# Row lists split by 64-row parts, and all-node blocks in layers 1 and 3, in a four-layer graph-attention kernel

## The chip, the cores and the metric

The kernel runs as one program on one core of a Trainium2 chip. The time of a run is the device time in microseconds, and a kernel's time is the median of its runs. The kernel before took 2251.94 us (three runs, 2251.93 to 2260.22). One execution was also profiled, and the profile's span, from the first to the last instruction, is 2249.3 us.

The engines are named as the profile names them: PE (TensorE matmuls) and PEld (its weight loads), DVE (VectorE), ACT (ScalarE), POOL (GpSimd, which here issues the indirect gathers) and SP (the queue of the plain DMAs).

## The reference

There are 4096 nodes of 256 features, and an adjacency matrix with density 1/256 plus the diagonal. Four graph-attention layers follow each other, each with a residual sum and a layer norm. Cut to what matters, layer 0 is:

```
h = (x @ W.T) in 4 heads of 64
e[i, j] = leaky_relu(alpha_src[i] + alpha_dst[j], 0.2)
attn = softmax over j of (e where adj[i, j] else -inf)
x = layernorm(x + concat over heads of attn @ h)
```

Layer 1 is the same with other weights. Layer 2 has 2 heads of 128. Layer 3 has two attentions, one of e and one of -e; both weigh x itself, the results are multiplied by a weight matrix, and an elu follows. All layers use the same adjacency.

## The kernel before

**Row tiles and lists.** The rows are worked on in 32 tiles of 128 (P = 128, NT = 32). A tile does not visit all 4096 nodes. While layer 0 runs, the generator `lists` (lines 293 to 486) finds for each row tile the nodes that are a neighbour of at least one of its 128 rows. `Block.prepare` loads the adjacency of four row tiles and turns it into bytes; `Block.places` counts where each node goes in the list; `Block.pack` compares an iota with these places (L440, one DVE operation for each of 31 node tiles) and multiplies the one-hot result with the mask on PE (L446), which moves mask columns and node numbers into up to 13 groups of 128 nodes. A fixed table, WINDOW, tells for each node tile which groups it may reach. The masks go to the DRAM tensor `maskC` and the node numbers to `idx`. A flag records whether anything fell outside; if it did, `dense_layers` computes everything again after the packed program.

**A sparse row tile.** `RowTile.load` issues the loads of a tile in two halves of 7 groups: the row factors S, the mask, the tile's own nodes (a plain DMA) and 13 indirect gathers by POOL (L647), each of which fetches one projected row for each of 128 nodes. The first six gathers read only nodes below MIX * 128 (MIX = 17). `RowTile.half` then computes the weights of 7 groups: for layers 0 and 1 one head's exponential comes as a product of two factors on DVE (L704, L708) and the three others from ACT (L712, an Exp with the node's term as bias); one DVE operation for two heads applies the lower bound and the mask (L681), with the mask copied into PSUM ahead of it (L666). The matmuls follow. Layers 0 and 1 (L724) load the 65 gathered value columns as weights and stream 128 rows, so the sums stand transposed; `copy` (L749) and `back` (L757) turn them. Layers 2 and 3 (L727) load the 128 x 128 weights and stream 129 or 257 value columns. `finish` and `norm` divide, add the residual and normalize.

**Projections.** `Projection` makes the next layer's rows: transposes (L543), products (L557), terms and values (L575 to L583), the row terms' transposition (L589).

**All-node blocks.** The table WHOLE names blocks of four row tiles that take no list: blocks 3, 7 and 6 in layer 2 and block 7 in layer 3. `whole_rows` goes through all 32 node tiles for them, with ACT exponentials of 128 x 512 (L1016), a DVE masking (L1017) and matmuls (L1027).

**The order.** There is no scheduler that moves work between steps: `Layer.part`, `half_alone`, `half_with_whole` and `close` write out the order in which each engine gets its instructions, and every engine works its queue in order. `half_with_whole` puts after each half some units of the all-node work (one unit is one node tile), spread evenly over the layer's halves by `whole`. `run` asks `lists` for one more row tile after each half tile of layer 0, ten tiles ahead (LEAD), and for the first 14 tiles' lists during layer 0's projections.

**Buffers.** Gathered rows stand in two pools: g0 with 16 and g1 with 14 buffers of two groups each. PSUM's eight banks are shared out in pools: ptwo (2 + 2), pair0 (2), pair1 (1) and pair2 (1, the mask copies).

## Time and profile before

| what | value |
|---|---|
| median of the runs | 2251.94 us |
| span of the profiled execution | 2249.3 us |
| PE busy | 2014.0 us (90%) |
| DVE busy | 1786.6 us (79%) |
| ACT busy | 1737.9 us (77%) |
| POOL busy | 1494.4 us (66%) |
| indirect gathers (L647) | 1456, mean 1017 ns |
| moved | 492.99 MB, mean 219 GB/s |

A busy share is that of the engine over the whole span, and the stages differ: layer 0 with the lists takes until about 784 us, layer 1 until 1347, layer 2 until 1763, layer 3 the rest. In a line of the view by stretches the columns are the stretch, its length, the busy time of each engine with its instructions, the granted TensorE clock, and the DMA share and rate. In a line of a timeline they are start, duration, engine, line, operation, tiles and count; in brackets stands how long the engine was idle before and what ended that. An f32 matmul is two records of the profile.

### The profile page before, as it was taken

The page shows a single profiled execution, that of the slowest core. Times are in us where ns is not written, and L with a number is a line of the kernel's source. Part 1 is how long each engine was busy: PE and PEld are TensorE (multiplying, and loading weights), DVE is VectorE, ACT ScalarE, POOL GpSimd, SP SyncE. Part 2 cuts the span into 40 slices and gives each one's busy share as a digit, 9 for nine tenths or more (in the row PEclk, how much of TensorE's full clock was granted, in tenths as well). Part 3 has the DMA queues.
Part 4 walks back from the last instruction along what each step waited for, and adds up shares of the span by engine and source line. Part 5 has one row for each costly group of instructions (what it writes and reads, how often), then busy time and mean ns, then how long its engine had stood idle before and what let it go on. Part 6 is the DMA issues. An engine that isn't in the chain of part 4 may idle for free. (4 is left out here: it accounts for less than half of the span.)

```text
span 2249.3 us, 49137 instructions
## 1 busy us (share of the span) xinstructions
PE 2014.0 (90%) x15689; PEld 1834.3 (82%) x15689; DVE 1786.6 (79%) x5060; ACT 1737.9 (77%) x4989; POOL 1494.4 (66%) x1597
## 2 busy tenths in 40 slices
PE   4878889989999969988899898989999999999995
PEld 2658788878899859988888798989998888788784
DVE  2889899999999959987988886887876566566566
ACT  4778988988789859987888776987876677667664
POOL 2107655656677777777777777777773477777773
PEclk7999999999999989999999999999999999999998
DMA  8879877777566665666665666777777688888884
GB/s 284 258 245 360 272 219 250 254 247 228 146 170 191 174 202 168 182 175 175 173 185 162 172 167 171 226 209 223 223 227 225 200 282 280 249 284 270 262 248 130
DMA packets 250319, 492.99 MB, mean 219 GB/s; under 512 B 44385, under 2 KB 156610, under 8 KB 249666
## 3 DMA queue, kind: packets, MB, share of 16 engines
q0 software_dynamic: 81536, 245.30, 38.3%
q1 hardware_dynamic: 163906, 240.26, 33.3%
q10 hardware_dynamic: 4608, 4.20, 0.5%
q8 instruction: 126, 2.06, 0.4%
q14 instruction: 143, 1.17, 0.2%
HBM read 437.05 MB, written 52.54 MB: 218 GB/s over the span
## 5 line engine op out<-in xcount | busy, mean ns | idle before, releaser
L647 POOL DMA_INDIRECT G<-vals,idx x1456 | 1480.7, 1017 | 715.7 <-issue 221.1
L712 ACT ACTIVATE w<-S,G 128x128 f32<-128x128 f32 x3248 | 1001.6, 390 | 140.6 <-DMA G<-vals,idx 101.6
L724 PE MATMUL bank<-w,G 128*65 128x128 f32 x7168 | 837.8, 276 | 59.7 <-DVE w L681 59.3
L724 PEld LDWEIGHTS bank<-w,G 128*65 128x65 f32 x7168 | 798.7, 140 | 69.9 <-DVE w L681 68.4
L681 DVE SCALAR_TENSOR_TENSOR w<-w,bank 128x1792 f32<-128x1792 f32 x256 | 514.6, 2013 | 13.4 <-ACT w L712 11.2
L727 PE MATMUL bank<-G,w 128*128 128x257 f32 (+1 forms) x2660 | 490.8, 342 | 25.7 <-ACT z L1102 13.6
L727 PEld LDWEIGHTS bank<-G,w 128*128 128x128 f32 x2660 | 431.9, 195 | 73.2 <-ACT z L1102 16.4
L1027 PE MATMUL bank<-vw,pw 128*128 128x129 f32 (+1 forms) x2048 | 298.5, 301 | 3.7 <-issue 2.3
L1027 PEld LDWEIGHTS bank<-vw,pw 128*128 128x128 f32 x2048 | 273.6, 191 | 20.1 <-issue 2.8
L690 ACT ACTIVATE w<-S,G 128x128 f32<-128x128 f32 x385 | 137.8, 393 | 136.8 <-DMA G<-vals,idx 90.0
L440 DVE TENSOR_SCALAR oh<-iota,place 128x256 bf16<-128x256 f16 (+2 forms) x992 | 221.8, 298 | 9.4 <-PE bank L446 9.1
L704 DVE TENSOR_TENSOR w<-S,G 128x256 f32<-128x256 f32 x384 | 151.9, 416 | 69.9 <-DMA G<-vals,idx 66.5
L446 PE MATMUL bank<-mk,oh 128*128 128x132 fp8e4 x2336 | 192.1, 226 | 13.8 <-ACT cm L453 7.0
L557 PE MATMUL bank<-wext,xT 128*128 128x268 f32 (+3 forms) x640 | 176.9, 409 | 16.9 <-ACT xT L548 14.1
L446 PEld LDWEIGHTS <-oh 128*128 128x128 bf16 x2336 | 146.9, 99 | 50.4 <-DVE oh L440 12.7
L385 ACT ACTIVATE mk<-raw 128x1024 uint8<-128x1024 int32 x128 | 130.5, 1051 | 28.0 <-DMA raw<-in_adjB_dram 27.7
L557 PEld LDWEIGHTS bank<-wext,xT 128*128 128x128 f32 x640 | 117.2, 200 | 36.0 <-ACT xT L548 16.9
L1017 DVE SCALAR_TENSOR_TENSOR pw<-pw,mw 128x512 f32<-128x512 f32 x192 | 127.6, 689 | 18.2 <-ACT pw L1016 17.5
L1016 ACT ACTIVATE pw<-Sw,d 128x512 f32<-128x512 f32 x192 | 133.2, 711 | 7.5 <-PE bank L1027 7.0
L714 DVE SCALAR_TENSOR_TENSOR w<-w,mk 128x896 f32<-128x896 f32 x80 | 86.6, 1086 | 41.1 <-ACT w L712 37.9
L1024 DVE TENSOR_TENSOR pw<-pw,mw 128x512 f32<-128x512 f32 x64 | 43.6, 691 | 85.4 <-ACT pw L1023 48.0
L692 DVE TENSOR_TENSOR w<-w,mk 128x896 f32<-128x896 f32 x55 | 60.0, 1091 | 59.5 <-ACT w L691 58.2
(140 smaller groups left out, 1563.3 us busy)
## 6 DMA issues: line engine op xcount, KB each, us to landing
raw<-in_adjB_dram SPq DMA_DIRECT2D x128, 512.0 KB
mk<-maskC SPq DMA_DIRECT2D x112, 231.0 KB
G<-vals,idx POOLq DMA_INDIRECT x1456
S<-edge SPq DMA_DIRECT2D x64, 256.0 KB
vw<-vals SPq DMA_DIRECT2D x96, 129.0 KB
xp<-y SPq DMA_DIRECT2D x96, 128.0 KB
y<-xp SPq DMA_DIRECT2D x96, 128.0 KB
mw<-maskW SPq DMA_DIRECT2D x20, 528.0 KB
```

Of the source, the lines that this page charges most:

```text
L440: nc.vector.tensor_scalar(oh[:, :n * P], iota[:, :n * P], self.place[:, it, j:j + 1], None, op0=ALU.is_equal)
L446: nc.tensor.matmul(accs[b][:, s * MC:(s + 1) * MC], oh[:, (k - a) * P:(k - a + 1) * P], mk[:, j, it, :].bitcast(FP8), start=touches[b][0] ...
L557: nc.tensor.matmul(pp[:, :c1 - c0], self.xT[:, k, :], wext[:, k, c0:c1], start=(k == 0), stop=(k == KT - 1 and brow is None))
L647: nc.gpsimd.indirect_dma_start(out=self.place(pos), out_offset=None, in_=sh["v"][n][:NODES[t], :], in_offset=bass.IndirectOffsetOnAxis(ap= ...
L681: nc.vector.scalar_tensor_tensor(pair, pair, LEAST, mh2, op0=ALU.max, op1=ALU.mult)
L690: nc.scalar.activation(w[0][:, k, :], S[:, 0, :], AF.Relu, bias=d(k, 0))
L704: nc.vector.tensor_tensor(w[h][:, k:k + 2, :], S[:, h:h + 1, :].to_broadcast([P, 2, P]), dd[:, :, V + T + h:V + T + h + 1].to_broadcast([P ...
L712: nc.scalar.activation(w[h][:, k, :], S[:, h, :], AF.Exp, bias=d(k, h))
L724: nc.tensor.matmul(accs[0][:Wd, h * P:(h + 1) * P], v, w[h][:, k, :], **how)
L727: nc.tensor.matmul(a, w[h][:, k, :], v, **how)
L1016: nc.scalar.activation(p, S[:, h], AF.Exp, bias=d)
L1027: nc.tensor.matmul(accs[it][:, c:c + Wd], p[:, it, :], v[:, c:c + Wd], start=(j == 0 and h == heads[0]), stop=(j == NT - 1), skip_group_ch ...
```

## The change

The list of a row tile is split by the two 64-row parts of the tile. A node that only the upper 64 rows need goes into the upper part of a *pair* unit, a node that only the lower 64 rows need into the lower part; a node that both need, or that does not fit, goes into a *mixed* unit. There are 5 pair units, each with 128 nodes for either part, and 3 mixed units. With the tile's own nodes a row tile has 9 units (U) of 128 x 128 weights instead of 14, and still 13 gathers.

```diff
-NG = 13
-NP = NG + 1
+HP = P // 2
+NPAIR = 5
+NMIX = 3
+NPACK = NPAIR + NMIX
+NU = NPACK + 1
+NP = 2 * NPAIR + NMIX
+HALF = 7
+FIRST = 3
+UNITS = (1 + FIRST, NPACK - FIRST)
+FULL = ((0,), tuple(range(NPAIR - FIRST, NPACK - FIRST)))
+PAIRS = (tuple(range(1, 1 + FIRST)), tuple(range(NPAIR - FIRST)))
...
-MIX = 17
+MIX = 23
...
-WHOLE = ((), (), (3, 7, 6), (7,))
+WHOLE = ((), (7, 6), (3, 7, 6), (7, 6))
```

`places` now sorts the nodes into three classes and computes places for each, with some 34 DVE operations a block; `pack` compares with an iota of up to 640 elements, since a node tile may reach pair units and mixed units:

```diff
-                    nc.vector.tensor_scalar(oh[:, :n * P], iota[:, :n * P], self.place[:, it, j:j + 1], None,
-                                            op0=ALU.is_equal)
-                    for k in range(a, a + n):
+                    nc.vector.tensor_scalar(oh[:, :len(ks) * P], iota[:, :len(ks) * P], self.place[:, it, j:j + 1],
+                                            None, op0=ALU.is_equal)
+                    for i, k in enumerate(ks):
```

In `half` the exponentials and factor products of a pair unit are done for 64 rows each with the part's own nodes, the maskings cover 4 or 5 units instead of 7, and all layers load the weights and stream the values. A 64-row part writes its own 64 partitions of the accumulator. `copy` and `back` go.

```diff
-        for h in heads:
-            for k in range(HALF):
...
-                v = G[k][:, h * Wd:(h + 1) * Wd]
-                if n < 2:
-                    nc.tensor.matmul(accs[0][:Wd, h * P:(h + 1) * P], v, w[h][:, k, :], **how)
-                else:
-                    a = accs[h][:, :Wd] if n == 3 else accs[0][:, h * Wd:(h + 1) * Wd]
-                    nc.tensor.matmul(a, w[h][:, k, :], v, **how)
+        for t, heads in enumerate(turns):
+            for us in (FULL[half], PAIRS[half])[::-1 if t == 1 and (half == 1 or n < 3) else 1]:
+                for h in heads:
+                    for u in us:
+                        for rows, g in parts[u]:
+                            a = accs[h][rows, :Wd] if n == 3 else accs[0][rows, h * Wd:(h + 1) * Wd]
+                            nc.tensor.matmul(a, w[h][:, u, rows], g[:, h * Wd:(h + 1) * Wd],
...
```

A new generator, `whole_heads`, does the all-node blocks of layer 1. It writes the exponential as the larger of a row factor and a node factor (the rest of the product is in the values), so that a weight is one DVE operation, and has no exponential per node tile. The row factors R stand in two PSUM banks (`pfloor`). Of two heads at a time, one loads weights and streams values, the other loads values and streams weights, and is turned at the end:

```diff
+                for h in (up, flat):
+                    R[h] = prog.bank(prog.pfloor)
+                    Sh = S[:, h].rearrange("p t i -> p (t i)")
+                    if h < A:
+                        nc.scalar.activation(R[h], Sh, AF.Exp, scale=-1.0, bias=sh["shift30"])
+                        nc.vector.tensor_scalar(R[h], R[h], HUGE, None, op0=ALU.min)
...
+                    for h in (up, flat):
+                        p[h] = prog.dp.tile([P, BT, P], F32, name="pw")
+                        nc.vector.scalar_tensor_tensor(p[h], R[h].rearrange("p (t i) -> p t i", t=BT), c[:, j, h:h + 1], mj,
+                                                       op0=ALU.max, op1=ALU.mult)
...
+                    for it in range(BT):
+                        nc.tensor.matmul(bu[:, it * Wd:(it + 1) * Wd], p[up][:, it, :],
+                                         v[:, up * Wd:(up + 1) * Wd], start=j == 0 and it == 0, **how)
+                        nc.tensor.matmul(bf[:Wd, it * P:(it + 1) * P], v[:, flat * Wd:(flat + 1) * Wd],
+                                         p[flat][:, it, :], start=j == 0 and it == 0, **how)
```

The buffers of gathered rows become larger and fewer, and while layer 1 runs its projections have one PSUM bank:

```diff
-        self.g0 = self.pool("g0", 16)
+        self.g0 = self.pool("g0", 4)
...
-        self.g1 = self.pool("g1", 14)
+        self.g1 = self.pool("g1", 4)
...
-        self.prog.banks = self.prog.ptwo[1] if self.n in (0, 2) else self.prog.pthree
+        self.prog.banks = self.prog.ptwo[1] if self.n in (0, 2) or self.closing else self.prog.pone
```

A buffer now holds 7 groups of layers 0 to 2 or 4 of layer 3. The sizes of the norm groups of layer 1 change, and layer 1 ends in the way in which layers with all-node blocks end (`close` starts all-node units of the next layer ahead of its first half).

## The prediction

> **What bounds the kernel now.** I read the busy times by stretch first, cut where one layer's gathers end and the next layer's begin (about 172, 784, 1347 and 1763 us), with one stretch inside the list building of layer 0.

> ```profile
> core 0: us, PE busy (x) PEld busy (x) DVE busy (x) ACT busy (x) POOL busy (x), PEclk, DMA share, GB/s
> 20.00:172.00 152.00, 108.11 (x956) 80.98 (x955) 113.42 (x466) 108.05 (x258) 16.15 (x58) 0.85 0.83 271
> 260.00:580.00 320.00, 286.10 (x2877) 260.65 (x2875) 314.45 (x943) 277.78 (x825) 196.05 (x193) 0.99 0.72 232
> 784.00:1347.00 563.00, 500.04 (x4196) 467.41 (x4194) 471.88 (x1083) 457.26 (x1538) 428.44 (x442) 0.97 0.63 176
> 1347.00:1763.00 416.00, 388.43 (x3055) 371.44 (x3055) 318.30 (x895) 317.06 (x857) 286.61 (x262) 0.98 0.73 212
> 1763.00:2249.00 486.00, 449.86 (x2028) 389.45 (x2026) 294.88 (x914) 314.90 (x668) 347.48 (x339) 0.96 0.80 249
> ```

> While lists are built DVE is full (314 of 320). Layers 2 and 3 are PE's (93%). In layer 1 no engine looks full, so I read POOL's timeline there, and who waited for whom.

> ```profile
> 1007.41 0.95 POOL L647 DMA_INDIRECT G<-vals,idx  x1 [0.30 <-issue]
> 1008.66 0.95 POOL L647 DMA_INDIRECT G<-vals,idx  x1 [0.30 <-PE bank L724]
> 1009.92 0.95 POOL L647 DMA_INDIRECT G<-vals,idx  x1 [0.30 <-issue]
> 1011.17 0.95 POOL L647 DMA_INDIRECT G<-vals,idx  x1 [0.31 <-issue]
> ```
> ```profile
> DVE w L704 <- DMA G<-vals,idx: 50.0, 26, 3.5
> ```

> A gather starts every 1.255 us: 0.95 busy and 0.30 of issue, whatever else runs. 13 of them are 16.3 us a row tile, and layer 1's 32 tiles, like layer 0's last eight, go at 16.4. Layer 1 is POOL's queue.

> The price of a matmul is read from starts in the PE timeline and in the chain; an f32 matmul is two records.

> ```profile
> 1006.74 6.28 PE L724 MATMUL bank<-w,G 128*65 128x128 f32 x56
> ...
> 1014.46 0.46 PE L757 MATMUL bank<-ident,aT 65*128 65x65 f32 x4
> ```
> ```profile
> 1488.73 1.50 PE L1027 MATMUL bank<-vw,pw 128*128 128x129 f32 x12
> 1490.07 0.27 PE L589 MATMUL bank<-ident,row 128*1 128x128 f32 x1
> 1490.18 0.38 PE L543 MATMUL bank<-ident,y 128*128 128x128 f32 x2
> 1490.40 1.84 PE L727 MATMUL bank<-G,w 128*128 128x129 f32 x15
> ```
> ```profile
> 1848.61 6.07 PE bank L727 x28
> 1854.68 1.73 PE bank L1027 x8
> ```

> 6.28 for 56 records (layers 0 and 1) is 0.112 with the tail, 0.109 from start to start; 1488.73 to 1490.07 for 12 is 0.112 at 129 columns; 6.07 for 28 is 0.217 at 257 columns (layer 3). A weight load hides under the record ahead in all of them. A 65-column record is seen only as a transpose, about 0.065 from start to start.

> **The change, part by part.**

> *Lists (layer 0).* A row tile still gathers 13 times, but packs into 8 units instead of 13. Per list tile the built program has 118 PE records for 73, and the same 31 DVE compares, wider: 640 elements in 341 of 992, 512 in 248, 384 in 279, 256 in 124. The forms before take 0.249, 0.291 and 0.316 us at 128, 256 and 384 elements, so about 0.35 and 0.38 at 512 and 640; consecutive DVE operations overlap by 0.07, so 31 compares go from 7.0 to 8.3 us. The placing of a block goes from 9 DVE operations to some 34, 13 of them 256 wide (0.42): 1.4 to 8.2 us a block, 0.35 to 2.05 a tile. The two halved reductions and the index arithmetic add 0.2. That is **+3.3 us of DVE a list tile.**

> *Sparse tiles of layers 0 and 1.* The maskings L681 take 2.01 at 1792 elements; with 0.69 at 512 (L1017) that is 1.03 ns an element, so 1.22 at 1024 and 1.48 at 1280: net of overlap 7.8 to 5.1 a tile. Factor products 2.5 to 1.5, mask copies 0.6 to 0.5. **-3.8 us of DVE a tile.** ACT has the same 42 exponentials, 30 of them half as wide, and loses the 0.57 copy of the transposed sums; four transposes go from PE.

> *Layer 0's sum.* In the middle stretch +3.3 and -3.8 meet on the full engine: 22 tiles by -0.5 = **-11 us**. At the start there are 14 lists and hardly a sparse tile: 14 by 3.3 = 46 us of DVE, of which the 39 us in which DVE idles between 20 and 172 can hide a part; PE gets 14 by 45 records by 0.06 = 38 more beside it. Bounds +15 to +60; I take **+35**. The last eight tiles stay at POOL's 16.4: nothing.

> *Layer 1.* Eight tiles leave POOL: 24 by 16.3 = 391 us is its new floor, so another engine is late next. PE: a sparse tile has 16 full-unit matmuls (128 weight columns, 65 streamed) and 40 of 64 weight columns. The first are bounded by 0.055 (half of 0.109, as half the columns stream) and 0.112 (L1027, same load of 128 x 128); I take 0.112, as that load has to be made. The second lie between half of 0.109 and 0.109; I take 0.065, the transpose's. 32 by 0.112 + 80 by 0.065 = 8.8 us a tile for 12.2 + 0.4 now; 24 tiles 211. Projections 2.1 by 32 = 67. The two all-node blocks: 512 matmuls with 128 weight columns (0.112 a record) and 512 of 128 streamed columns (0.109): 226, or 200 if a short record's load hides under a long one. PE 478 to 504. DVE: 14.7 - 3.8 = 10.9 by 24 = 262, the eight tiles' endings 24, 256 maskings of 512 elements 170 (0.665 net, L1017) to 190 (the row factors now lie in PSUM; 256-wide L1121 from PSUM takes 0.06 more than L1126 from SBUF), factors 8: 464 to 484. Both run side by side 93% full, as in layers 2 and 3: 563 becomes **510 (-53)**. The 18 us in which PE stands at 822 to 840 now can take all-node work, but that work first waits for the last projected tile, so I count nothing there.

> *Layer 2.* POOL's floor 326. Its sparse matmuls are 40 half-width and 16 full ones a tile. Two consecutive half-width ones stand in the two 64-column halves of the array (the built program places them at columns 0 and 64). No row shows such a pair. Its bounds: one after the other, 0.110 a record as now (no gain), or side by side, two for the time of one. Then 16 by 0.112 + 40 by 0.055 = 4.0 for 6.3 us; 20 tiles by 2.3 = 45 off PE's 388; POOL's 16.3 a tile leaves **-28** of it.

> *Layer 3.* 24 sparse tiles for 28, two all-node blocks for one (a block is 32 x 4 x 2 x 2 by 0.217 = 111). PE now 28 by 12.15 + 111 = 451. Side by side: 24 by (16 by 0.217 + 40 by 0.109 = 7.8) + 222 = 409; one after the other: 24 by 12.15 + 222 = 514. POOL's floor is 391. The bytes stay (about 137 MB), and at the 310 GB/s of the busiest stretches take 440. So **460 (-26)** side by side, **550 (+64)** one after the other. I take side by side for both layers: the two parts use disjoint columns and the trace shows loads hidden under any earlier record; both ends stay for the range.

> [...]

> *Changing array shape* costs by the rows nothing or 0.09: L589 has a 32-column tile, and starts 0.11 after the L1027 record, with the next 0.11 after it, so no pause; L560, a tile of few rows, starts 0.31 after a record of 0.22. The change alternates full and half-width matmuls some three times a half row tile, 136 halves in layers 1 to 3: 0 to 37 us. I take 0, as L589 too is a column tile.

> [...]

> **Sum.** 2249.3 + 35 - 11 - 53 - 28 - 26 = 2166; the median shown is 2.6 above the profiled span, so **2170 us**.

> **Rivals.**
> (a) *The halves don't run side by side.* The place is layer 3's PE, +64 instead of -26, and layer 2 gains nothing: +35 - 11 - 53 + 64 = 2284 + 2.6, about **2290, slower**. It decides once a pair in layer 3 takes more than about 1.7 times one record (83 of gain against a swing of 118). For it: no row shows overlap of two matmuls. Against: nothing in the program orders the two.
> (b) *The vector side of layer 1 and the longer lists eat the gain.* DVE at 484 and PE at 504 wait for each other through few buffers and one PSUM bank for projections; if layer 1 stays near 550 and the start takes 50: about **2222**. For it: layer 1's DVE is fuller than layer 3's.
> (c) *Weight loads overlap too and the start hides:* layer 1 near 480, start +5: about **2105**.
> (d) A list that overflows its window sends the program through the dense path after all, thousands of us; windows of 4.5 deviations leave that under 1 in 100.

> **Chances.** Forecast 0.50, (a) 0.25, (b) 0.15, (c) 0.09, (d) 0.01. The forecast's own range is 2125 to 2215 (start bounds, layer-1 bounds, drain). To leave out two in ten, the range goes half into (a) and (c): 2095 to 2285. Faster by over 0.5% (about what a measurement can tell from no change): 0.49 + 0.09 + 0.11 of (b) + 0.02 of (a) = 0.71; within 0.5% 0.07; slower 0.22.

> **What would show it.** Right: 28-record halves of layer 3 near 4 us instead of 6.07; layer 1's row tiles about 21 us apart with PE and DVE above 90%; POOL with idle time in layer 1; 1300 gathers still 1.255 apart; first sparse tile of layer 0 some 35 us later, its middle pace still 21 to 22. Wrong: half-width records of layer 3 starting every 0.217; pauses at each change between full and half-width; POOL still back to back in layer 1; DVE idle in the list stretch.

## The result, and the profile after

The changed kernel takes **2342.68 us** (median of four runs, 2332.35 to 2351.3) where the kernel before, run beside it, takes 2256.08: a ratio of **1.038, 95% interval 1.036 to 1.041, slower**. The forecast was 2170 and the range 2095 to 2285, so both the size and the sign were wrong. The profiled execution took 2332.35 us, its span is 2330.6.

In some sessions the engines idled on their own issue (PE for 312 to 472 us, for 0 to 26 in all others) and the kernel before itself took 2742 to 2772 us, where two of the same chips ran it in some 2256 at another time; runs from there are marked "stalling session" and are compared only with the kernel before beside them.

First the busy times by stretch of the changed kernel: list building, layer 0's middle, and layers 1, 2 and 3. (The cuts at 900, 1460 and 1856 are the first gathers of layers 1, 2 and 3. Of the cuts of before, 784 is layer 1's first gather too, but 1347 is layer 1's last finished row tile and 1763 lies 20 us behind layer 2's: there the next layer's first gathers had begun at 1313 and 1681.)

```profile
core 0: us, PE busy (x) PEld busy (x) DVE busy (x) ACT busy (x) POOL busy (x), PEclk, DMA share, GB/s
20.00:223.00 203.00, 141.88 (x1492) 116.56 (x1491) 146.38 (x562) 110.86 (x250) 17.42 (x13) 0.82 0.71 235
300.00:700.00 400.00, 335.22 (x3820) 306.26 (x3817) 341.99 (x1093) 255.99 (x843) 203.72 (x210) 0.74 0.62 192
900.00:1460.00 560.00, 504.58 (x5228) 447.33 (x5226) 456.59 (x1121) 310.80 (x1179) 304.12 (x313) 0.92 0.63 180
1460.00:1856.00 396.00, 356.32 (x3000) 327.36 (x3000) 286.38 (x871) 295.09 (x857) 274.22 (x260) 0.94 0.71 205
1856.00:2330.00 474.00, 437.92 (x2345) 322.35 (x2345) 279.41 (x906) 325.17 (x739) 320.39 (x313) 0.96 0.83 263
```

The second line is the surprise. In layer 0's middle, VectorE was 98% busy before and is 85% busy now, PE's share fell only from 89 to 84%, and the clock that PE is granted fell from 0.99 to **0.74**. Busy PE time is stretched by a low clock: the changed kernel's list records (L510) start 113 ns apart in the median where the trace's clock record says 0.5, and 59 where it says 1.0. So PE's 335 us hold, by estimate, only some 248 us of work at full clock (335 x 0.74). The page's clock row shows the stretch by eye: sevens and sixes where the kernel before had nines.

```profile
PEclk7999999999999989999999999999999999999998
PEclk8987777677678677799999997899999999999998
```

(The first row is the kernel before, the second the changed one.) A half row tile shows what that means: 28 short records of layer 0 in the PE timeline.

```profile
505.78 3.89 PE L819 MATMUL bank<-G,w 128*128 128x65 f32 x28 [2.59 <-DVE w L763]
509.60 0.38 PE L662 MATMUL bank<-ident,row 128*4 128x128 f32 x1
509.91 3.89 PE L819 MATMUL bank<-G,w 128*64 128x65 f32 x28
```

These are 3.89 us, after a wait of 2.59 for the masking. The waits of that stretch (columns: us in total, times, longest):

```profile
ACT cm L516 <- PE bank L510: 60.8, 23, 8.3
PEld bank L819 <- DVE w L763: 51.6, 29, 3.0
PE bank L819 <- DVE w L763: 45.8, 29, 2.8
DVE oh L504 <- PE bank L510: 44.7, 31, 2.3
```

PE waits for VectorE's masks (L763), VectorE waits for PE to free a compare buffer (L504), and ScalarE's list copies wait for PE too. No engine is full. In the same part of the kernel before (230 to 600 us) the two lines of PE and VectorE waiting for each other were 27 and 4 us:

```profile
PE bank L724 <- DVE w L681: 27.2, 24, 2.3
DVE oh L440 <- PE bank L446: 4.3, 1, 4.3
```

Where the 81 us of span came from, by the first and last row tile's finish in each layer (worked out from the ends of L1117 and L1127 before, L1264 and L1274 after):

| stretch | before | after | difference |
|---|---|---|---|
| start to layer 0's first finish | 210.6 | 262.6 | +52 |
| layer 0, first to last | 601.6 | 656.2 | +55 |
| layer 0's last to layer 2's first (all of layer 1) | 569.8 | 595.2 | +25 |
| layer 2, first to last | 360.7 | 331.3 | -29 |
| into layer 3 | 58.0 | 65.7 | +8 |
| layer 3, first to last | 437.2 | 410.6 | -27 |
| end | 11.4 | 9.0 | -2 |

### The profile page after: what moved, and what is told of

Its sections match the earlier page's. It is cut to its first block, busy times and chain, and to the rows that moved or that the text cites. A ratio compares the mean times of both kernels' runs of the same rounds, so it can differ in the third digit from the quotient of the medians.

```text
span 2330.6 us, 54083 instructions
## 1 busy us (share of the span) xinstructions
PE 2013.2 (86%) x18383; PEld 1731.8 (74%) x18383; DVE 1730.0 (74%) x5248; ACT 1498.1 (64%) x4596; POOL 1312.8 (56%) x1374
## 4 chain that ended last, share of the span: by engine, by line
PE 44%; DVE 10%; DMA 6%; POOL 5%; ACT 4%; issue 3%; SPq 0%; DVEq 0%; POOLq 0%; ACTq 0%
PE bank L819 18%; PE bank L1106 13%; DMA G<-vals,idx 5%; POOL G L714 4%; PE bank L630 4%; PE bank L1176 3%; PE bank L1174 3%; DVE w L763 3%; ACT w L805 2%; DVE pw L1170 1%; ACT pw L1095 1%; PE bank L633 1%; PE bank L616 1%; DVE w L801 1%; PE bank L510 1%
## 5 line engine op out<-in xcount | busy, mean ns | idle before, releaser
L714 POOL DMA_INDIRECT G<-vals,idx x1300 | 1307.2, 1006 | 980.6 <-issue 420.8
L819 PE MATMUL bank<-G,w 128*64 128x65 f32 (+5 forms) x8708 | 853.7, 301 | 129.6 <-DVE w L763 101.8
L819 PEld LDWEIGHTS bank<-G,w 128*64 128x64 f32 (+1 forms) x8708 | 702.7, 182 | 283.4 <-DVE w L763 120.1
L805 ACT ACTIVATE w<-S,G 128x64 f32<-128x64 f32 (+1 forms) x2912 | 783.4, 351 | 128.9 <-DMA G<-vals,idx 106.3
L1106 PEld LDWEIGHTS bank<-vw,pw 128*128 128x128 f32 x2560 | 375.6, 194 | 50.9 <-issue 15.6
L763 DVE SCALAR_TENSOR_TENSOR w<-w,bank 128x1024 f32<-128x1024 f32 (+1 forms) x224 | 301.6, 1347 | 69.0 <-ACT w L805 68.5
L504 DVE TENSOR_SCALAR oh<-iota,place 128x640 bf16<-128x640 f16 (+3 forms) x992 | 284.0, 351 | 61.0 <-PE bank L510 60.6
L510 PE MATMUL bank<-mk,oh 128*128 128x136 fp8e4 x3782 | 264.1, 233 | 5.6 <-ACT cm L516 3.6
L510 PEld LDWEIGHTS <-oh 128*128 128x128 bf16 x3782 | 249.2, 103 | 12.8 <-DVE oh L504 3.4
L1170 DVE SCALAR_TENSOR_TENSOR pw<-bank,cw,mw 128x512 f32<-128x512 f32 x256 | 182.8, 740 | 1.3 <-PE bank L1176 0.7
L1174 PE MATMUL bank<-vw,pw 128*128 128x65 f32 x1024 | 149.9, 267 | 21.5 <-DVE pw L1170 21.5
L1176 PE MATMUL bank<-pw,vw 128*65 128x128 f32 x1024 | 163.8, 278 | 0.0
L773 ACT ACTIVATE w<-S,G 128x64 f32<-128x64 f32 (+1 forms) x329 | 104.8, 352 | 85.8 <-DMA G<-vals,idx 48.0
L1174 PEld LDWEIGHTS bank<-vw,pw 128*128 128x128 f32 x1024 | 138.7, 195 | 23.4 <-issue 21.7
```

What stands on the lines that cost most here:

```text
L504: nc.vector.tensor_scalar(oh[:, :len(ks) * P], iota[:, :len(ks) * P], self.place[:, it, j:j + 1], None, op0=ALU.is_equal)
L510: nc.tensor.matmul(accs[b][:, s * MC:(s + 1) * MC], oh[:, i * P:(i + 1) * P], mk[:, j, it, :].bitcast(FP8), start=touches[b][0] == (j, k), ...
L714: nc.gpsimd.indirect_dma_start(out=self.place(half, k), out_offset=None, in_=sh["v"][n][:N if half else MIX * P, :], in_offset=bass.Indire ...
L763: nc.vector.scalar_tensor_tensor(pair, pair, LEAST, mh2, op0=ALU.max, op1=ALU.mult)
L805: nc.scalar.activation(w[h][:, u, rows], S[:, h, rows], AF.Exp, bias=d(g, h))
L819: nc.tensor.matmul(a, w[h][:, u, rows], g[:, h * Wd:(h + 1) * Wd], start=half == 0 and u == 0 and (n == 3 or h == turns[0][0]), stop=half ...
```

## The experiments

I held three theories. **A:** in layer 0 PE has less to do, so it is granted a lower clock, and the slow PE now holds the others. **B:** the longer lists (more records, wider compares, longer placing) are the price. **C:** the ring of eight compare buffers is. For layer 1, **D:** its single PSUM bank for projections holds it; against it **E:** PE's and VectorE's own work does.

**The changed kernel once more**, as the row to hold the others against.

> The changed kernel once more, as the row that the other kernels of this call are held against. On a chip that issues as in the first pair of traces: 2332 to 2351 us against 2252 to 2260, layer 0's middle at a granted clock near 0.74. On one where engines idle on their own issue (the kernel before at some 2755): between 2940 and 3000, and about 0.72 as clock; the kernel with layer 1's projections on three banks (2871, 1.039 of the kernel before) is then the faster by some 90 us, all of it between layer 1's first and last finish. If the single bank cost nothing, both differ by less than 20.

Measured: 2337.82, ratio 1.037 (1.031 to 1.042), first layer-0 finish 261.8, layer 0 first to last 659.2, all of layer 1 596.8, as in the first trace. It says nothing of the three-bank kernel of a stalling session; that follows below.

**More work for PE in layer 0** (theory A).

```
+        if n == 0:
+            for i in range(8):
+                nc.tensor.matmul(accs[0][:, 3 * P:], sh["ident"], sh["ident"], start=half == 0 and i == 0, stop=False,
+                                 skip_group_check=True)
```

> The changed kernel with eight more matmuls (two records each, identity by identity, 1.75 us at full clock) at the end of each half row tile of layer 0, into columns of the sums' bank that nothing reads. That gives PE 3.5 us more of a row tile, so that its work at full clock (0.74 of 339 us over 17 tiles) is about as much as in the kernel before. If the clock that is granted follows what PE has to do, and the low clock is what slows layer 0's middle (theory A), the clock there rises from 0.74 to 0.9 or more and the pace falls from 23.7 towards 22: 20 to 40 us less. If the clock is a consequence of waits, PE gets later: pace 24 to 27, 10 to 70 us more, clock under 0.85.

(In the program they stand ahead of the half's own matmuls, not behind them.) Measured: **2295.51**, ratio 1.018 (1.009 to 1.027): 42 us less by doing more. Layer 0's first to last finish went from 656 to 605, almost the 602 of before; all of layer 1, which the edit doesn't touch, took 13 longer (610). The stretch and the waits of this kernel:

```profile
300.00:700.00 400.00, 369.61 (x4880) 345.37 (x4881) 379.99 (x1225) 285.74 (x964) 244.37 (x239) 0.93 0.68 207
```
```profile
PE bank L823 <- DVE w L763: 17.6, 20, 1.9
DVE oh L504 <- PE bank L510: 10.6, 12, 1.5
```
```profile
501.51 2.17 PE L823 MATMUL bank<-G,w 128*128 128x65 f32 x28 [0.65 <-DVE w L763]
```

The clock is 0.93, VectorE is 95% busy again, its wait for PE to free a compare buffer fell from 45 to 11 us, and the 28 records take 2.17. PE's wait for the masks fell from 46 to 18 us, in part because the matmuls of nothing stand in that wait. Theory A's forecast came true in clock and pace (23.6 to 21.0 us a row tile over the same 16 tiles, where the kernel before has 20.9) and in time (42 less for the forecast 20 to 40); neither B nor C allows a gain from added work.

**Shorter lists** (theory B). Windows are cut to 77 pieces for 122; this leaves neighbours out.

```
-WINDOW = windows()
+WINDOW = [(a + (n > 2), min(n, 2 - j % 2), j // 11, 1) for j, (a, n, e, x) in enumerate(windows())]
```

> Windows cut down to 77 pieces over all source tiles for 122, so that a list tile has about the PE records of the kernel before and compares of 256 to 384 elements; the flag is held at zero. It leaves out neighbours whose place falls outside the cut window. Placing, layout and sparse tiles are as changed. If the longer lists are the price of layer 0 (theory B), the start comes back to some 15 us over the kernel before and the middle's pace from 23.7 to 21 or less: 60 to 90 us less than the changed kernel on a chip that issues as in the first traces, more on a slower one. If the clock that PE is granted is the cause (theory A), PE with still less to do is granted no more (0.74 or under) and the time falls by less than 30.

Measured: 2300.95, ratio 1.020 (1.017 to 1.024): 37 less, between the two forecasts. The start gave back 13 us (first finish 248.9), the middle 27. The stretch of this kernel:

```profile
300.00:700.00 400.00, 328.34 (x3291) 284.77 (x3290) 330.93 (x1151) 265.48 (x881) 218.09 (x221) 0.70 0.65 195
```

With lists as short as before, VectorE is still only 83% busy and the clock is lower still, 0.70. So B is a part (37 us less while the clock fell), and the middle keeps a loss of some 30 us over before (632 for 602) that the length of the lists does not explain; the longer placing is still in it.

**Sixteen compare buffers** (theory C): `pool("oh", 8)` becomes `pool("oh", 16)`.

> The changed kernel with 16 buffers for the compares of the lists in place of 8. If the ring of 8 is what makes VectorE wait for PE (46 us in the middle of layer 0, theory C), those waits go and the middle's pace falls by 1 to 2.5 us a tile: 20 to 55 us less. If the ring only shows that PE is late, the waits move to the masking or to the copies of the lists, and the time stays within 12.

Measured: 2318.89, ratio 1.028 (1.018 to 1.038). Layer 0's start is 7 us and its middle 15 to 18 shorter.

```profile
PE bank L819 <- DVE w L763: 40.1, 34, 2.4
DVE t L525 <- ACT cm L516: 16.4, 11, 3.1
DVE oh L504 <- PE bank L510: 15.3, 12, 2.8
```

VectorE's wait for the ring falls from 45 to 15 us, but half of that returns as a wait for the list copies, and the clock is 0.77. The ring carries a part of the loss; that a slow PE shows through it fits these waits and is not shown by them alone.

**Three banks for layer 1's projections** (theory D): the row factors go to SBUF.

```
-        self.prog.banks = self.prog.ptwo[1] if self.n in (0, 2) or self.closing else self.prog.pone
+        self.prog.banks = self.prog.ptwo[1] if self.n in (0, 2) or self.closing else self.prog.pthree
...
-                    R[h] = prog.bank(prog.pfloor)
+                    R[h] = prog.bk.tile([P, BANK], F32, name="Ru" if h == up else "Rf", bufs=2)
```

> The row factors of layer 1's all-node maskings in SBUF, and layer 1's projections on the three turning banks (theory D, one bank for projections holds layer 1). If D holds: the copies that wait for the projection bank go (98 us of it in the changed kernel), layer 1's paces of 18 to 23 fall towards 18, and layer 1's first to last finish falls from 476 by 15 to 60 us. If layer 1 is set by the work of PE (459 of 510 busy) and VectorE itself, it falls by less than 10.

Measured: 2321.91, ratio 1.029 (1.020 to 1.038). Layer 1's first to last finish fell from 476 to 465.5, all of layer 1 from 597 to 584. That is below D's band of 15 to 60 and a little above E's limit of 10: E for the most part, with 10 to 12 us for the bank: the maskings are no faster from SBUF (L1170 takes 743 ns on average, 740 in the changed kernel). In the stalling session the same kernel had a layer 1 some 90 us shorter than two others with one bank (587 for 678); where the engines issue freely that size does not hold.

**No all-node blocks in layer 1, one in layer 3**, lists as changed: WHOLE and GROUPS as before, three banks.

> Lists split by 64-row parts as changed, but all-node blocks as in the kernel before: none in layer 1, one in layer 3. Layer 0 as in the changed kernel. If layer 1's all-node blocks gain what POOL no longer gathers, layer 1 (first to last finish) goes back from 476 to some 500 to 530, since 32 tiles by 16.4 are 525, and the gaps around it (56 and 62) shrink to 44 to 55; layer 3 to POOL's 28 by 16.4 = 460 for 411. Altogether 40 to 90 us slower than the changed kernel. If the blocks cost layer 1 as much as they save, it is within 20 of the changed kernel.

Measured: 2330.28, ratio 1.033 (1.024 to 1.042), as fast as the changed kernel. Layer 3 lost what was forecast (441 for 411 us), but **layer 1 got shorter by leaving its blocks out**: 573.5 for 596.8, and 584.4 with blocks and three banks, so about half of the 23 us is the single bank's. Layer 0's first to last finish was shorter too, 642 for 659, though the edit takes nothing from it but small copies on VectorE (4 us); why stays open, and the ring's 15 to 18 us above are no more than that. POOL's queue in this kernel, where layer 1's gathers end and layer 2's begin (at 1413.15):

```profile
1410.65 0.94 POOL L714 DMA_INDIRECT G<-vals,idx  x1 [0.30 <-issue]
1411.90 0.95 POOL L714 DMA_INDIRECT G<-vals,idx  x1 [0.30 <-issue]
1413.15 0.95 POOL L714 DMA_INDIRECT G<-vals,idx  x1 [0.30 <-issue]
```

and the same place in the changed kernel:

```profile
1369.17 0.95 POOL L714 DMA_INDIRECT G<-vals,idx  x1 [0.30 <-issue]
1459.58 1.31 POOL L714 DMA_INDIRECT G<-vals,idx  x1 [89.46 <-DVE pw L1096]
```

In the changed kernel POOL is done 43 us earlier (1369 for 1412) and then idles 89.5: what it is spared comes back as one wait for layer 2's first sources.

**The first half's gathers read 17 tiles for 23**: what that wait depends on. It leaves out tiles 17 to 22 in the first half's units.

```
-        nc.vector.memset(limit[:, :2 * FIRST], float(MIX * P - 1))
+        nc.vector.memset(limit[:, :2 * FIRST], float(17 * P - 1))
...
-                out=self.place(half, k), out_offset=None, in_=sh["v"][n][:N if half else MIX * P, :],
+                out=self.place(half, k), out_offset=None, in_=sh["v"][n][:N if half else 17 * P, :],
```

> The gathers of a row tile's first half read rows 0 to 2175 (17 tiles) for 0 to 2943 (23 tiles), with the indices clamped to it: it leaves out, in the first half's units, nodes of tiles 17 to 22 (they read row 2175 in their place). Everything else as changed. If POOL's idle time ahead of layers 2 and 3 comes from waiting for the 23rd projected tile, that wait goes (89 to under 15 us ahead of layer 2), layer 1's last finish to layer 2's first falls by 20 to 30 us and the same into layer 3 by 5 to 10: 25 to 40 us less in all. If what is late there is PE's and DVE's own all-node work, POOL's idle time goes and the time stays within 10.

Measured: 2312.81, ratio 1.026 (1.022 to 1.029): 25 less, at the lower end of the forecast. The 89 us gap is gone; layer 1's last finish to layer 2's first fell from 63 to 45 us, into layer 3 from 66 to 60, while layer 1 itself, first to last, took 10 longer.

**Neighbouring parts not in turn** (do halves run side by side?). All upper parts of a head come first, then all lower ones.

> The same matmuls, but of each head and group of mixed units first all upper and then all lower parts, so that no two neighbours stand in different halves of the array; each still loads 64 weight columns. If neighbours in different halves do run side by side and that is what layers 2 and 3 gain by, layer 3 (first to last finish) grows by 60 to 105 us and layer 2 by up to 30, and layer 1 by up to 40 where PE is late: 80 to 170 more in all. If they run one after the other anyway, and the gain comes from elsewhere, the time stays within 15.

Measured: 2361.80, ratio 1.047 (1.044 to 1.051): 24 more, between the two forecasts (within 15, or 80 to 170). But the kernel did not do what its expectation says. In layer 3 of the changed kernel, starts of half-width records come in pairs, 6 to 7 ns apart, and a pair every 0.217 us (2005.445 and 2005.451, 2005.662 and 2005.668). In this kernel they should have come singly, as the three upper matmuls (six records) stand ahead of the three lower ones in the program. The starts form two rows of six instead: 2034.012, 2034.281, 2034.497, 2034.714 and 2034.931 go on in one row, and 2034.503, 2034.771, 2034.987 begin the other. The trace does not name a record's column half; if the first row is the six upper ones, PE started records for the free half while earlier ones for the other half had not started. So side by side is shown by the starts, the order only inferred; what serial halves would cost was not measured.

**Half of the kernel before's sparse matmuls in layer 0** (does less work for PE help at all?), in two stalling sessions. It leaves out half of layer 0's neighbours.

```
-            for k in range(HALF):
+            for k in range(0, HALF, 2 if n == 0 else 1):
```

> The kernel before with only every other group's matmuls in layer 0: it leaves out half of layer 0's neighbours, and halves PE's sparse work there (229 us of the 333 in its middle), with nothing else changed. If the granted clock follows what PE has to do, it falls from 0.98 to 0.8 or less in layer 0's middle, and PE's waits for VectorE and VectorE's for PE grow; the time stays within 25 of the kernel before or is longer. If PE was late in any part of layer 0, and the clock stayed, 10 to 40 us less.

Measured: 2769.48 beside 2753.3 in the first, 2772.57 beside 2758.63 in the second, ratio 1.006 (1.002 to 1.009): no faster, at a clock of 0.77 and 0.75 over most of layer 0. It fits A; since these engines also stalled on issue, it alone would not decide.

**A combination.** The single results point to a kernel with split lists and layer 3's two blocks, but no blocks in layer 1, 16 compare buffers and the eight matmuls of nothing; and, since a list was expected to cost more alone at the start than between row tiles, `LEAD = 6` for 10. Two versions of it, with ten and with six lists ahead, ran first in a stalling session:

> Split lists as changed, layer 3's two all-node blocks as changed, but none in layer 1 (its projections on the three banks); 16 compare buffers; eight matmuls of nothing ahead of each half's own in layer 0. If the losses are separate: the kernel without layer 1's blocks (2330), less 30 for layer 3 (441 for 411), 42 for the clock and 10 to 19 for the buffers: 2235 to 2250, just under the kernel before. If the clock and the buffers are one loss: 2250 to 2270, no faster.

> As e14_no_l1_blocks, but six lists instead of ten are packed before layer 0's first row tile. A list costs about 11 us alone at the start (79.8 to 137.8 us for five), and between row tiles the difference of the middle's pace and the end's, 21.5 - 16.4 = 5: four lists moved are 15 to 30 us less. If the first row tiles then wait for their lists, nothing or 10 us more.

Measured there: 2819.17 and 2816.32 beside 2758.63, ratios 1.021 (1.017 to 1.024) and 1.020 (1.017 to 1.024). Six lists ahead only moved work: layer 0's first finish came 42 us earlier (245 for 288) and its first to last finish took 44 longer (918 for 874). The second was then run again:

> The kernel of e15_lead6 once more (no all-node blocks in layer 1 and its projections on three banks, two in layer 3, 16 compare buffers, eight matmuls of nothing a half in layer 0, six lists ahead). Where the kernel before takes some 2256: 2330 - 30 (layer 3's second block) - 42 (clock) - 10 to 19 (buffers) - 15 to 30 (fewer lists ahead) = 2210 to 2235, 1 to 2% under the kernel before. If clock and buffers are one loss and the lists only move: 2250 to 2265. Where engines stall on issue and the kernel before takes some 2755: 1.02 of it again.

Measured: **2235.24** beside 2253.98, ratio **0.990 (0.987 to 0.993): 1% faster than the kernel before**, at the upper end of the forecast. Layer 0's first finish comes at 222 and its last at 848 (812 before, 919 changed), layer 3 takes 412. In layer 1 of this kernel POOL paces again, at 16.4 us a row tile, and PE's clock is 0.68 without harm:

```profile
240.00:680.00 440.00, 403.65 (x5307) 378.38 (x5305) 416.23 (x1330) 325.36 (x1057) 272.21 (x256) 0.93 0.72 229
830.00:1356.00 526.00, 416.81 (x3894) 352.49 (x3894) 336.11 (x885) 372.25 (x1447) 399.55 (x416) 0.68 0.64 172
```

Three of the cures together in the changed kernel (eight matmuls of nothing a half, 16 buffers, three banks), in a stalling session:

> The changed kernel with three of the single edits together: eight matmuls of nothing a half in layer 0, 16 compare buffers, and layer 1's row factors in SBUF with three banks for its projections. Separate losses: 2338 - 42 - 19 - 16 = 2261, the kernel before's time. If clock and buffers are one loss (VectorE waits for a PE that is slow): 2275 to 2285.

Measured: 2873.76 beside 2758.63, ratio 1.040 (1.035 to 1.044). Without the changed kernel beside it this doesn't say how the three add up; that stays open.

**Four early runs** in two stalling sessions, with six matmuls of nothing, 16 buffers, lists only, and three banks, took 2977.57, 2953.72, 2882.26 and 2870.89, 1.081, 1.073, 1.047 and 1.039 of the kernel before. The changed kernel did not run beside them, so they decide nothing alone; all four were repeated above (the first with eight matmuls). The first of them, for one, had expected:

> The changed kernel, and in layer 0 six more f32 matmuls of 128 x 128 on PE ahead of each half's own, into unused columns of the sums' bank: 12 x 0.22 = 2.6 us of PE a row tile, that nothing reads. Theory A (layer 0's middle is slow because PE, with less to do, is granted 0.74 of its clock, and the slow PE then holds the compares' buffers): the granted clock between 223 and 750 us rises over 0.9, a tile's pace falls from 23.7 towards 21.5 us, the time falls by 30 to 60 us to 2275 to 2300. Theory B (the longer list work itself, 118 records and wider compares, is the price): PE has more to do, the pace stays at 23.7 or grows by up to 2.6, the time is 2330 to 2390.

There the clock rose to 0.79 only, with PE idle on issue.

## Why the prediction was wrong, step by step

**Layer 0's middle, "22 tiles by -0.5 = -11": measured +55. This step failed first.** VectorE's terms were about right: maskings L763 take 1347 ns on average for 1.22 and 1.48 forecast, compares L504 351 ns. Its condition, that VectorE stays the full engine, did not hold. PE's work has no term in that sum: I took it as something that lies beside, at the price of a full clock. The change spares PE in the sparse tiles, the clock goes to 0.74, and PE then delivers sums and frees compare buffers later than VectorE needs them. With the clock held up by matmuls of nothing the middle is +3 over before: the sum of VectorE's durations was off by about 14 us, and the clock, which had no term, cost about 50.

**The start, +35 (bounds 15 to 60): measured +52.** The mechanism was right, the term too small. VectorE idles 57 of 203 us now (39 of 152 before): no idle time took in any of the added 46.

**Layer 1, "510 (-53)": measured +25 over all of layer 1. This step failed too.** The layer's own first to last finish fell by 14 (490 to 476), but the way into it grew by 13 (44 to 57) and the way out by 27 (36 to 63). Between last finishes (layer 0's to layer 1's) it is -1: by no cut -53. PE's work was not priced too low: 478 to 504 us forecast, 505 busy measured at a clock of 0.92, some 464 at full clock; the L1170 maskings took 183 us for 170 to 190, though not by what reading PSUM was to cost them (743 ns from SBUF, 740 from PSUM). But "both run side by side 93% full" held only in the middle (975 to 1390: PE 95%, VectorE 87%, clock 0.98). At 900 to 975 us PE was 65% busy and stood once for 21 us, until the first all-node masking at 952.5, 22 us behind the last projection of layer 0's rows (I had counted nothing there, and should have counted a loss):

```profile
PE bank L1174 <- DVE pw L1170: 21.2, 1, 21.2
```

At 1390 to 1460 the last tiles and projections follow each other at a clock of 0.73; and POOL, no longer late, waits 89.5 us for the 23rd projected tile, where it went straight on before. Against the true alternative, sparse tiles all through, two all-node blocks in layer 1 cost 23 us, about half of it by the single bank that their row factors leave to the projections. A floor that is removed is worth no more than the distance to the next one with its ramps.

**Layers 2 and 3, -28 and -26: measured -29 and -27 from first to last finish. The mechanism was right; the sizes are right in part by luck.** Halves do run side by side, and rival (a) did not happen: halves of layer 3 take 4.06 or 4.68 us from start to start, near the forecast 4, for 6.07 before; the second kind, with its tail:

```profile
2003.57 4.84 PE L819 MATMUL bank<-G,w 128*128 128x257 f32 x28
```

But the way into each layer grew (by 27 and by 8). Between last finishes, layer 2 gained 3 us (396 to 394) and layer 3 with the end 21 (507 to 485); without the 89 us wait (17 tiles for 23) layer 2 takes 374 by this measure, a gain of 22, so the rest of its gain went into layer 1's ending. And layer 3's PE was busy for 438 us where the sum said 409; the 51 us that the forecast of 460 had on top of PE's sum covered it.

**Changing array shape, 0 taken, bounds 0 to 37.** The rows now show the price. In the layer-3 half above, a half-width record after a full one starts 0.310 us later for 0.217 and the next of its half 0.268 later; after the last pair the next two full ones come at 0.310 and 0.321. The half is 4.68 us from first start to the next group's, and 20 slots of 0.217 make 4.34: 0.34 for two changes. The other half, with four changes, is 4.06, and 16 slots make 3.47: 0.59. That is some 0.16 a change, more than L560's end of the bounds (0.09), and 22 us in layer 3's 48 halves; I took 0. The range of the forecast names a drain; no run shows one, only that the records behind a change start later by these amounts. L589's row, by which I took 0, is of a 32-column tile and did not carry over.

**The rivals.** Of (b), which let layer 1 and the lists eat the gain, the place was right and the price far too small; it ended on the faster side. No rival had PE's clock in it, though the view I read first showed it: in the kernel before's list building PE is 71% busy and its clock is 0.85. This table, worked out from stretches shown here and in the prediction, is the row that was missing. Work is busy time by clock, as a share of the stretch.

| stretch | PE busy | clock | PE's work at full clock |
|---|---|---|---|
| before, layer 0's middle | 0.89 | 0.99 | 0.89 |
| before, list building | 0.71 | 0.85 | 0.60 |
| changed, layer 0's middle | 0.84 | 0.74 | 0.62 |
| cut windows, layer 0's middle | 0.82 | 0.70 | 0.57 |
| eight more matmuls, layer 0's middle | 0.92 | 0.93 | 0.86 |
| combination, layer 1 | 0.79 | 0.68 | 0.54 |
| changed, layer 3 | 0.92 | 0.96 | 0.89 |

In these rows the clock is 0.93 or higher with 0.86 and more of a stretch full of work, and 0.68 to 0.85 with 0.54 to 0.62, and the busy share hides it. The table alone does not say which of the two sets the other, as the clock is a factor of the work; the added matmuls do, which raised it from 0.74 to 0.93.

The mean clocks here are mixtures of two values. The list records show it (in the changed kernel they start 59 ns apart in the median and 113 at the 95th percentile), and so do the clock records of the traces before and after, from which PEclk is printed: they hold 1.0 and 0.5 only, each, but for the last of a trace, for a multiple of 3.41 us. Held against PE's busy time in the changed kernel, the clock fell 50 times, each time after an interval of 3.41 us in which PE was busy for 69% or less (35% on average), and rose 49 times, each time after one in which PE was busy for 93% or more; not every full interval raised it (44 of 78). In the kernel before, the 23 falls came after at most 55% and the 22 rises after at least 85%. Where between these shares the clock would turn, no run shows. Between 300 and 700 us the changed kernel's clock fell 16 times and stayed down for 13.2 us on average; with the eight matmuls of nothing 7 times for 7.8, in the kernel before once for 3.4. The 16 falls stand in a stretch where PE's 29 waits for masks are 1.6 us on average and 2.8 at most, so gaps as short as these went with them.

## What to carry to other kernels

Where a change spares PE work in a stretch that another engine bounds, work out busy time by granted clock first: if PE falls to some 0.6 of the stretch (0.62 in layer 0's middle here, at a clock of 0.74), price its remaining records at the low clock and ask who waits for them; here that cost some 50 us. Count the gaps too, as each fall of the clock in that middle lasted some 13 us. A stretch that one queue paced with nothing else late (the combination's layer 1 under POOL, 16.4 us a row tile) bore a clock of 0.68 without loss, and work moved off that queue gained only what the next layer's first sources allowed (89.5 us of POOL's idle time ahead of layer 2). An engine's total is a floor and not a time: add the ramp at which its work may begin and the chain with which the layer ends.
